# Two groups of leftover products in one PE block: eight PSUM banks in layer 1 of a CIN kernel

## The chip, the cores and the metric

The kernel runs on one core of one Trainium2 chip. The metric is the device time of one execution in microseconds. The kernel before took 2045.8 us (median of four runs, 2045.0 to 2046.51). All times below are microseconds unless another unit stands beside them. Engines are named as the profile names them: PE is the matrix engine, PEld its weight loads, DVE the vector engine (VectorE), ACT the scalar engine (ScalarE), POOL is GpSimd, SP is the queue that issues most loads.

## The reference

Two layers of a compressed interaction network over 4096 rows of 32 fields with 16 elements each. Each layer forms all products of two sets of fields, element by element, multiplies them by a weight matrix, adds a bias, and normalises each output channel over rows and elements. Half of the first layer's channels feed the second layer; everything else is summed over the elements.

```python
def _cin_layer(out, x, W, b, gamma, beta):
    r, _, e = x.shape
    h = jnp.einsum('rne,rfe->rnfe', out, x).reshape(r, -1, e)
    h = jnp.einsum('rce,oc->roe', h, W) + b[None, :, None]
    return _batchnorm(h, gamma, beta)      # mean and variance over rows and elements
h1 = _cin_layer(x, x, W1, b1, g1, beta1)   # W1: 128 x (32*32)
out, direct1 = (h1[:, :64], h1[:, 64:])
direct2 = _cin_layer(out, x, W2, b2, g2, beta2)   # W2: 128 x (64*32)
return jnp.concatenate([direct1, direct2], axis=1).sum(axis=-1)
```

Everything is in 32-bit floats.

## The kernel before, in words

The 65,536 sites (row and element) are cut into 128 tiles of 512. Layer 1 runs over the tiles, the last four (`ENDING`) in a part of their own; layer 2 runs over 64 chunks of two tiles, each in four stages.

**Layer 1, one tile.** A product x_i * x_j occurs twice, so only half of the products is formed, with the two weights added beforehand. 512 of them make the main part: two loads `a` and `b` on SP (512 KB each, four buffers each), one DVE multiplication into `z` (128 x 2048, L387, four buffers), four PE matmuls of 128 rows (L428). 16 products per tile are left over. The leftovers of eight tiles (`GROUP`) share one load `r` (L279) and one DVE product `zr` (L373), one buffer each; 16 rows of `zr` belong to each tile. Two tiles share a strip of 32 rows, and weights with 16 rows of zeros (`w1_sb[rows, 4]` or `[rows, 5]`) pick the one that is meant. `add_leftovers` (L376 to L382) issues four matmuls of 32 rows, one for each of four tiles, each into another bank.

**Order on PE.** At every fourth tile t four banks are taken from the pool `psum` (six banks); the block of leftovers begins the sums of tiles t to t+3, and the four main matmuls of each tile end them. Only the first two tiles (`FIRST`) begin with their main part and end with the leftovers.

**Eviction.** `finish(t)` (L342 to L361) is called one tile later: ACT evicts a bank three times (L352, L355, L358: all channels to `e`, the kept half to `h`, the direct half to `ed`), DVE takes statistics of `e` (L115, two `e` buffers), after each second tile also a sum of `ed` (L364), and ACT's queue stores `h` to HBM. Two more banks (the pool `factors`) are free in layer 1.

**Work for later.** A table (`EARLY`, L205 to L214) puts at fixed tiles the loads, negations and sums that prepare layer 2: two loads `xs` (L190) in every 24 tiles, layer 2's first operands from tile 75 on. The layer 2 weights come at tile 6 and are combined at tile 20.

**Order of the instructions.** A scheduler sets the order of each engine, by the order of the program and its own estimate of times; each engine then runs its own in that order, and waits on semaphores for the others. `tc.issue_after` binds an instruction behind another. SP issues DMAs in order as well, and a DMA waits for its buffer and for the one issued eight DMAs before.

**The beginning.** Tile 0 is loaded in four quarters. ACT's queue loads the weights `w1` and their mirror `w1m`, 384 KB each; POOL adds them in four steps (L312), the first main weights first. Tiles 0 and 1 are multiplied in four chunks each (L396).

**The boundary.** The last four tiles take their kept half first (L461), whose statistics give the scale and shift (`keep`) of layer 2's input. The direct half follows on PE while these are worked out, and the leftovers of the last four tiles use the last `zr`.

**Layer 2.** In a stage DVE multiplies twice (L667), adds one `t2` half (L662); POOL makes the other `t2` half (L703) and two differences `t14` (L714); PE makes 32 matmuls (L698). `combine` is a generator that evicts a chunk's sums in steps; `next(steps)` puts one step into the order of ACT and DVE.

Of the kernel before, what the change touches and what calls it, by code (L numbers as in the profile page):

```python
# [38 lines left out]
FP = mybir.dt.float32  # L42
# [4 lines left out]
P = 128  # L47
# [20 lines left out]


@with_exitstack  # L70
def tile_cin(ctx: ExitStack, tc: tile.TileContext, xa, xb, xr, w1, w1m, w2, bn, out):
    nc = tc.nc

    const = ctx.enter_context(tc.tile_pool(name="const", bufs=1))
# [188 lines left out]
    with ExitStack() as one:  # L263
# [11 lines left out]
        def load_rem(g):  # L275

            r = rpool.tile([P, 2 * T], FP, tag="r", name="r")
            with tc.issue_after(loads[-1].ins) if loads else nullcontext():
                nc.sync.dma_start(r, bass.AP(xr.tensor, xr.offset + g * P * 2 * T, [[2 * T, P], [1, 2 * T]]))  # L279
            return r  # L280

        def load_main(t):
            a = lpool.tile([P, 2 * T], FP, tag="a", name="a")
            b = lpool.tile([P, 2 * T], FP, tag="b", name="b")

            def load(to, part, n):
                at = part * T
                if to is a:
                    at += xa.offset + t * FIELDS * 2 * T
                    source = bass.AP(xa.tensor, at, [[2 * T, FIELDS], [0, 4], [1, n * T]])  # L290
                else:
                    at += xb.offset + (t * WRAP + 2) * T
                    source = bass.AP(xb.tensor, at, [[T, FIELDS], [4 * T, 4], [1, n * T]])
                return nc.sync.dma_start(to[:, part * T : (part + n) * T], source)

            if t == 0:

                parts = ((a, 0, 1), (b, 0, 1), (b, 1, 1), (a, 1, 1))
            else:
                parts = ((a, 0, 2), (b, 0, 2))  # L300
            for part in parts:
                last = load(*part)
            loads.append(last)
# [12 lines left out]
        neg_sb = const.tile([P, 2, 2, KEEP], FP, tag="neg", name="neg_sb")  # L316
# [46 lines left out]
        def sum_direct(c):  # L363
# [4 lines left out]
                ALU.add,  # L368
            )

        def leftovers(r):
            zr = rpool.tile([P, T], FP, tag="zr", name="zr")
            nc.vector.tensor_tensor(zr, r[:, :T], r[:, T:], ALU.mult)  # L373
            return zr

        def add_leftovers(t, zr, begun=0):  # L376

            for k in range(4):
                rows = slice(32 * k, 32 * (k + 1))
                nc.tensor.matmul(  # L380
                    pss[t + k], w1_sb[rows, 4 + t % GROUP // 4, :], zr[rows, :], start=k >= begun, stop=k < begun
                )  # L382

        def multiply_main(z, a, b, k):

# [11 lines left out]

        ending = NT - ENDING
        main = [load_main(t) for t in range(FIRST)]
        r = load_rem(0)  # L400
        for t in range(NT - ENDING):
            s = t % GROUP
            if s == 4 and t + 4 < NT:
                r = load_rem(t // GROUP + 1)
            if FIRST <= t + 1 < NT:
                main.append(load_main(t + 1))
            if s == 0 and t > 0:
                zr = leftovers(r)
            z = zpool.tile([P, 2, 2, T], FP, tag="z", name="z")
            if t < FIRST:  # L410
                for k in range(2):
                    for j in range(2):
                        product = multiply_chunk(z, *main[0], k, j)
            else:

                for k in (slice(0, 1), slice(1, 2)) if t == FIRST else (slice(0, 2),):
                    product = multiply_main(z, *main[0], k)
            main.pop(0)
            if t == FIRST - 1:
                with tc.issue_after(product.ins):  # L420
                    zr = leftovers(r)
            if s % 4 == 0:
                for k in range(4):
                    pss[t + k] = psum.tile([P, T], FP, tag="ps", name="ps")
            if s % 4 == 0 and t > 0:
                add_leftovers(t, zr)
            for m in range(4):
                nc.tensor.matmul(  # L428
                    pss[t],
                    w1_sb[:, m, :],  # L430
                    z[:, m // 2, m % 2, :],
                    start=t < FIRST and m == 0,
                    stop=t >= FIRST and m == 3,
                )
            if t == FIRST - 1:
                add_leftovers(0, zr, FIRST)
# [23 lines left out]
        def matmul(ps, w, z, start, stop):  # L460
            queue("pe", lambda: nc.tensor.matmul(ps, w, z, start=start, stop=stop))  # L461
# [13 lines left out]
        def add_leftovers_halves(banks, zr, direct, begun):  # L475

            for k in range(ENDING):
                rows = slice(32 * k, 32 * (k + 1))
                to = banks[k][half_of[(k + direct) % 2]]
                matmul(to, w1_sb[rows, 5, half_of[direct]], zr[rows, :], k not in begun, k in begun)  # L480
# [219 lines left out]
    def sum_first(z):  # L700

        t2 = tpool.tile([P, 2, T], FP, tag="t2", name="t2")
        queue("pool", lambda: nc.gpsimd.tensor_tensor(t2[:, 0], z[:, 1, 0], z[:, 0, 0], ALU.add))  # L703
        return t2

    def sum_rest(z, b11, t2, by_q, by_k):
# [149 lines left out]
    for c in range(NC):  # L856
# [3 lines left out]
        for k, i in enumerate(STAGES):  # L860
# [148 lines left out]
```

## Time and profile before

| what | value |
|---|---|
| median of four runs | 2045.8 (2045.0 to 2046.51) |
| the profiled execution | 2045.3, span 2043.6, mean granted PE clock 0.998 |
| PE, DVE, POOL, ACT busy | 2027.4, 1958.7, 1486.9, 1185.4 |
| layer 1 up to the last four tiles | from 0 to 474.3 |
| the last four tiles | 474.3 to 490.7 |
| layer 2 on PE | 490.7 to 2025.9 |

The page's first part gives busy time and share of each engine. PE is busy 99% of the span, and the chain that ended last is PE's by 98%, so the time is the sum of PE's work and what little PE waits. A line of the timeline reads: start, duration, engine, line of the kernel, operation, output <- inputs, shapes, count, and in brackets how long the engine stood idle before and what released it. A line of the chain reads: start, duration, engine, output, line, count. A line of the windows gives for each engine the busy time and the number of instructions, then the granted clock, the mean busy share of the 16 DMA engines (a little over 1 when they are full) and GB/s.

### The profile page before, as it was taken

How to read it: one execution, taken by the hardware profiler on the slowest of the kernel's cores; microseconds unless marked ns; L12 is line 12 of the kernel's file. 1: busy time of each engine (PE TensorE's matmuls, PEld its weight loads, DVE VectorE, ACT ScalarE, POOL GpSimd, SP SyncE). 2: the span in 40 equal slices, each digit the busy share in tenths (PEclk: the TensorE clock that was granted, in tenths of full speed). 3: DMA queues.
4: the chain of work that ended last, by engine and by line, in shares of the span. 5: the costliest groups of instructions: out<-in, count | busy, mean ns of one | idle time of the engine just before them, and what ended most of it. 6: DMA issues, size and time to landing. Idle time of an engine off the chain costs nothing.

```text
span 2043.6 us, 24467 instructions
## 1 busy us (share of the span) xinstructions
PE 2027.4 (99%) x8500; PEld 888.8 (43%) x8500; DVE 1958.7 (96%) x1521; ACT 1185.4 (58%) x1914; POOL 1486.9 (73%) x525
## 2 busy tenths in 40 slices
PE   9999999999999999999999999999999999999997
PEld 3444444443344444444444444444444444444443
DVE  8998987998999999999999999999999999999997
ACT  4555554554566666655666656556656565566564
POOL 0000000002999999999999999999999999999996
PEclk9999999999999999999999999999999999999999
DMA  9999999996777777777776777777777677777761
GB/s 391 376 354 365 343 362 339 380 386 190 174 179 174 178 175 180 189 174 183 179 177 166 174 174 176 177 181 178 176 166 174 174 172 182 181 176 176 168 162 42
DMA packets 112380, 440.70 MB, mean 216 GB/s; under 512 B 13056, under 2 KB 13056, under 8 KB 103808
## 3 DMA queue, kind: packets, MB, share of 16 engines
q1 hardware_dynamic: 105840, 418.43, 73.9%
q10 hardware_dynamic: 6416, 20.72, 2.6%
q8 instruction: 66, 1.08, 0.2%
q14 instruction: 58, 0.48, 0.1%
HBM read 417.07 MB, written 22.02 MB: 215 GB/s over the span
## 4 chain that ended last, share of the span: by engine, by line
PE 98%; DVE 1%; issue 0%; POOL 0%; DMA 0%; ACT 0%; DVEq 0%; ACTq 0%; POOLq 0%
PE x L698 74%; PE ps L428 21%; PE ps L380 2%; PE ps L461 1%; DMA w1m_sb<-in_w1m 0%; POOL t L714 0%; DVE zz L667 0%; DVE d L934 0%; ACT u L659 0%; DVE both L662 0%; POOL t L703 0%; ACT both L659 0%; DVE d L833 0%; DVE t L662 0%; POOL w_sb L312 0%
## 5 line engine op out<-in xcount | busy, mean ns | idle before, releaser
L714 POOL TENSOR_TENSOR t<-zz,t 128x2048 f32<-128x2048 f32 (+1 forms) x260 | 1164.0, 4478 | 20.8 <-DVE t L662 1.0
L698 PE MATMUL x<-t,s_sb 128*64 128x512 f32 x2040 | 958.3, 592 | 0.4 <-POOL t L714 0.4
L698 PE MATMUL x<-zz,s_sb 128*64 128x512 f32 x2048 | 935.0, 592 | 0.0
L698 PE MATMUL x<-zz,w_sb 128*64 128x512 f32 x2056 | 760.5, 592 | 0.0
L703 POOL TENSOR_TENSOR t<-zz 128x512 f32<-128x512 f32 x255 | 326.3, 1280 | 516.1 <-DVE zz L667 515.8
L667 DVE TENSOR_TENSOR zz<-f,bx 128x2048 f32<-128x2048 f32 x255 | 582.4, 2284 | 19.7 <-ACT f L659 19.7
L659 ACT ACTIVATE f<-a,keep 128x512 f32<-128x512 f32 x512 | 398.4, 778 | 342.8 <-DVE zz L667 293.1
L667 DVE TENSOR_TENSOR zz<-f,b 128x2048 f32<-128x2048 f32 x255 | 582.5, 2284 | 0.1
L698 PEld LDWEIGHTS x<-t,s_sb 128*64 128x64 f32 x2040 | 279.2, 137 | 485.0 <-issue 456.8
L698 PE MATMUL x<-t,w_sb 128*64 128x512 f32 x1020 | 479.3, 592 | 0.0
L428 PE MATMUL ps<-z,w_sb 128*128 128x512 f32 x992 | 434.7, 596 | 1.7 <-POOL w_sb L312 1.5
L698 PEld LDWEIGHTS x<-zz,s_sb 128*64 128x64 f32 x2048 | 279.5, 137 | 245.9 <-issue 239.3
L387 DVE TENSOR_TENSOR z<-a,b 128x2048 f32<-128x2048 f32 (+1 forms) x127 | 288.0, 2269 | 43.2 <-DMA b<-in_xb 21.3
L428 PEld LDWEIGHTS ps<-z,w_sb 128*128 128x128 f32 x992 | 185.7, 190 | 249.2 <-issue 228.1
L698 PEld LDWEIGHTS x<-zz,w_sb 128*64 128x64 f32 x2056 | 239.4, 137 | 120.8 <-issue 118.9
L659 ACT ACTIVATE b<-zz 128x512 f32<-128x512 f32 x255 | 152.4, 598 | 187.2 <-DVE zz L667 187.2
L352 ACT ACTIVATE e<-ps,bn_sb 128x512 f32<-128x512 f32 x124 | 85.2, 687 | 215.7 <-PE ps L428 162.0
L662 DVE TENSOR_TENSOR t<-zz,b 128x512 f32<-128x512 f32 x255 | 173.4, 680 | 0.4
L698 PEld LDWEIGHTS x<-t,w_sb 128*64 128x64 f32 x1020 | 139.6, 137 | 0.0
L596 ACT ACTIVATE unread<-e,center 128x512 bf16<-128x512 f32 x122 | 86.2, 707 | 0.0
L358 ACT ACTIVATE ed<-ps,bn_sb 64x512 f32<-64x512 f32 x124 | 84.7, 683 | 2.4
L115 DVE BATCH_NORM_STATS2 stats<-e 128x6 f32<-128x512 f32 x124 | 84.9, 686 | 0.0
(103 smaller groups left out, 867.1 us busy)
## 6 DMA issues: line engine op xcount, KB each, us to landing
a<-h SPq DMA_DIRECT2D x256, 512.0 KB, 4.6
b<-in_xb SPq DMA_DIRECT2D x64, 1024.0 KB, 9.4
a<-in_xa SPq DMA_DIRECT2D x127, 512.0 KB, 7.0
b<-in_xb SPq DMA_DIRECT2D x127, 512.0 KB, 8.1
bx<-in_xb SPq DMA_DIRECT2D x64, 512.0 KB, 9.3
bx<-x SPq DMA_DIRECT2D x64, 512.0 KB, 10.9
h<-kept ACTq DMA_DIRECT2D x64, 256.0 KB, 5.7
r<-in_xr SPq DMA_DIRECT2D x16, 512.0 KB, 8.7
```

The source lines that it names most:

```text
L115: nc.vector.bn_stats(self.stats[:, self.at, :], h)
L352: nc.scalar.activation(e, ps, AF.Identity, bias=b1)
L358: done = nc.scalar.activation(ed[to, :], ps[KEEP:, :], AF.Identity, bias=b1[KEEP:])
L387: return nc.vector.tensor_tensor(z[:, k], a.rearrange("p (a t) -> p a t", a=2)[:, k].unsqueeze(2).to_broadcast([P, n, 2, T]), b.rearrange( ...
L428: nc.tensor.matmul(pss[t], w1_sb[:, m, :], z[:, m // 2, m % 2, :], start=t < FIRST and m == 0, stop=t >= FIRST and m == 3,)
L596: return nc.scalar.activation(unread, e[:, s], AF.Square, bias=center[:, s], accum_out=squares[:, s, c : c + 1])
L659: return queue("act", lambda: nc.scalar.activation(to, source, AF.Identity, **scale_bias))
L662: return dve(lambda: nc.vector.tensor_tensor(to, x, y, ALU.add))
L667: dve(lambda: nc.vector.tensor_tensor(z, a, b.rearrange("p (k q) t -> p k q t", k=2), ALU.mult))
L698: queue("pe", lambda: nc.tensor.matmul(self.of[x], w, b, start=start, stop=stop))
L703: queue("pool", lambda: nc.gpsimd.tensor_tensor(t2[:, 0], z[:, 1, 0], z[:, 0, 0], ALU.add))
L714: queue("pool", lambda: nc.gpsimd.tensor_tensor(t14[:, k, q], z[:, 2 + k.start : 2 + k.stop, q], twice[:, k, q], ALU.subtract))
```

## The change

**Leftovers of eight tiles in one block.** At tiles 8, 16, ..., 120 (and no longer at 4, 12, ...) `add_leftovers` is called twice: it ends the sums of tiles t-4 to t-1 and begins those of t to t+3. Tiles 8g+4 to 8g+7 therefore begin with their main matmuls and are complete only when the double block of the next group has run. Both fours use one `zr`; the host arranges `xr` anew, so that a group holds tiles 8g-4 to 8g+3, in 17 groups and not 16. Tiles 6 and 7 of each eight take their banks from `factors`, so layer 1 uses all eight banks.

**Later eviction.** `finish` is called four tiles after a tile and not one; near the end twice in one tile, so that it catches up.

**The end of layer 1.** The last four tiles need a load `r` (at tile 121) and a `zr` of their own.

**The beginning.** Tile 0 comes in two loads as every other tile. ACT's queue loads the main weights and their mirror in one DMA (512 KB), SP the leftovers' weights (256 KB) behind tile 1's loads. DVE adds the main weights in one instruction, POOL the leftovers' weights.

**Layer 2.** For the stage (0, 1) DVE and not POOL makes the first half of `t2`. In chunks 0 to 4 one `next(steps)` of the first stage moves from behind the next stage's first factor to ahead of it.

```diff
@@ load_main
-            if t == 0:
-                parts = ((a, 0, 1), (b, 0, 1), (b, 1, 1), (a, 1, 1))
-            else:
-                parts = ((a, 0, 2), (b, 0, 2))
...
+            nc.sync.dma_start(
+                a, bass.AP(xa.tensor, xa.offset + t * FIELDS * 2 * T, [[2 * T, FIELDS], [0, 4], [1, 2 * T]])
+            )
+            at_b = bass.AP(xb.tensor, xb.offset + (t * WRAP + 2) * T, [[T, FIELDS], [4 * T, 4], [1, 2 * T]])
+            loads.append(nc.sync.dma_start(b, at_b))
@@ weights
-        w1m_sb = zpool.tile([P, 6, P], FP, tag="z", name="w1m_sb")
-        nc.scalar.dma_start(w1_sb, w1)
-        nc.scalar.dma_start(w1m_sb, w1m)
-        for k in (slice(0, 1), slice(1, 2), slice(2, 4), slice(4, 6)):
-            nc.gpsimd.tensor_tensor(w1_sb[:, k], w1_sb[:, k], w1m_sb[:, k], ALU.add)
+        w1_both = zpool.tile([P, 2, 4, P], FP, tag="z", name="w1_both")
+        nc.scalar.dma_start(w1_both, w1)
         bn_sb = load_bn()
+        left_both = zpool.tile([P, 2, 2, P], FP, tag="z", name="left_both")
+        nc.vector.tensor_tensor(w1_sb[:, :4], w1_both[:, 0], w1_both[:, 1], ALU.add)
@@ leftovers and banks
+        def multiply_leftovers(zr, r):
+            return nc.vector.tensor_tensor(zr, r[:, :T], r[:, T:], ALU.mult)
+        def bank(t):
+            pool, tag = (psum, "ps") if t % GROUP < 6 else (factors, "f")
+            return pool.tile([P, T], FP, tag=tag, name="ps")
+        def ends_with_leftovers(t):
+            return t % GROUP >= 4 or t < FIRST
-        def add_leftovers(t, zr, begun=0):
+        def add_leftovers(t, zr):
             for k in range(4):
                 rows = slice(32 * k, 32 * (k + 1))
-                nc.tensor.matmul(
-                    pss[t + k], w1_sb[rows, 4 + t % GROUP // 4, :], zr[rows, :], start=k >= begun, stop=k < begun
-                )
+                last = ends_with_leftovers(t + k)
+                w = w1_sb[rows, 4 + (t + 4) % GROUP // 4, :]
+                nc.tensor.matmul(pss[t + k], w, zr[rows, :], start=not last, stop=last)
@@ the loop over tiles
         main = [load_main(t) for t in range(FIRST)]
+        nc.sync.dma_start(left_both, w1_left)
+        nc.gpsimd.tensor_tensor(w1_sb[:, 4:], left_both[:, 0], left_both[:, 1], ALU.add)
         r = load_rem(0)
...
-                    pss[t + k] = psum.tile([P, T], FP, tag="ps", name="ps")
-            if s % 4 == 0 and t > 0:
+                    pss[t + k] = bank(t + k)
+            if s == 0 and t > 0:
+                add_leftovers(t - 4, zr)
                 add_leftovers(t, zr)
...
-            if t > 0 and t < ending - 1:
-                evicted = finish(t - 1)
+            if t >= ending - 2:
+                evicted = finish(t - 2)
+            elif t >= ending - 4:
+                for done in range(2 * t - ending, 2 * t - ending + 2):
+                    evicted = finish(done)
+            elif t >= 4:
+                evicted = finish(t - 4)
+            if t == ending - 3:
+                r = load_rem(NT // GROUP)
...
-            if t == 0:
+            if t < 4:
                 continue
@@ the last four tiles
+            if k == 0:
+                zr = rpool.tile([P, T], FP, tag="zr", name="zr")
+                queue("dve", lambda: multiply_leftovers(zr, r))
@@ layer 2
-                t2 = sum_first(z)
+                t2 = sum_first(z, (c, k) == (0, 1))
...
+            if k == 0 and c < 5:
+                next(steps, None)
...
-            next(steps, None)
+            if k > 0 or c >= 5:
+                next(steps, None)
@@ the host
-    xr = np.stack([xt[:, :16], xt[:, 16:]], axis=2).reshape(NT // GROUP, GROUP // 4, 4, 16, 2, T)
+    xr = np.stack([xt[:, :16], xt[:, 16:]], axis=2)
+    xr = np.concatenate([xr[:4], xr, xr[-4:]]).reshape(NT // GROUP + 1, GROUP // 4, 4, 16, 2, T)
```

More of the change, by code (lines that the diff above doesn't have):

```diff
@@ L70, in tile_cin @@
 @with_exitstack
-def tile_cin(ctx: ExitStack, tc: tile.TileContext, xa, xb, xr, w1, w1m, w2, bn, out):
+def tile_cin(ctx: ExitStack, tc: tile.TileContext, xa, xb, xr, w1, w1_left, w2, bn, out):
     nc = tc.nc
@@ L284, in load_main @@
             b = lpool.tile([P, 2 * T], FP, tag="b", name="b")
[L286 to L290, printed above, removed]
-                else:
-                    at += xb.offset + (t * WRAP + 2) * T
-                    source = bass.AP(xb.tensor, at, [[T, FIELDS], [4 * T, 4], [1, n * T]])
-                return nc.sync.dma_start(to[:, part * T : (part + n) * T], source)
-            if t == 0:
-                parts = ((a, 0, 1), (b, 0, 1), (b, 1, 1), (a, 1, 1))
-            else:
-                parts = ((a, 0, 2), (b, 0, 2))
-            for part in parts:
-                last = load(*part)
-            loads.append(last)
+            nc.sync.dma_start(
[3 more added lines that the diff above has]
+            loads.append(nc.sync.dma_start(b, at_b))
             return a, b
         w1_sb = wpool.tile([P, 6, P], FP, tag="w1", name="w1_sb")
-        w1m_sb = zpool.tile([P, 6, P], FP, tag="z", name="w1m_sb")
-        nc.scalar.dma_start(w1_sb, w1)
-        nc.scalar.dma_start(w1m_sb, w1m)
-        for k in (slice(0, 1), slice(1, 2), slice(2, 4), slice(4, 6)):
-            nc.gpsimd.tensor_tensor(w1_sb[:, k], w1_sb[:, k], w1m_sb[:, k], ALU.add)
+        w1_both = zpool.tile([P, 2, 4, P], FP, tag="z", name="w1_both")
+        nc.scalar.dma_start(w1_both, w1)
         bn_sb = load_bn()
+        left_both = zpool.tile([P, 2, 2, P], FP, tag="z", name="left_both")
+        nc.vector.tensor_tensor(w1_sb[:, :4], w1_both[:, 0], w1_both[:, 1], ALU.add)
         w2_sb = const.tile([P, 16, P], FP, tag="w2", name="w2_sb")
@@ L369, in sum_direct @@
             )
+        def multiply_leftovers(zr, r):
+            return nc.vector.tensor_tensor(zr, r[:, :T], r[:, T:], ALU.mult)
         def leftovers(r):
             zr = rpool.tile([P, T], FP, tag="zr", name="zr")
[L373 removed]
+            multiply_leftovers(zr, r)
             return zr
[L376 removed]
+        def bank(t):
[4 more added lines that the diff above has]
+        def add_leftovers(t, zr):
             for k in range(4):
                 rows = slice(32 * k, 32 * (k + 1))
[L380 to L382 removed]
+                last = ends_with_leftovers(t + k)
+                w = w1_sb[rows, 4 + (t + 4) % GROUP // 4, :]
+                nc.tensor.matmul(pss[t + k], w, zr[rows, :], start=not last, stop=last)
         def multiply_main(z, a, b, k):
@@ L431, in tile_cin @@
                     z[:, m // 2, m % 2, :],
-                    start=t < FIRST and m == 0,
-                    stop=t >= FIRST and m == 3,
+                    start=ends_with_leftovers(t) and m == 0,
+                    stop=not ends_with_leftovers(t) and m == 3,
                 )
             if t == FIRST - 1:
-                add_leftovers(0, zr, FIRST)
-            if t > 0 and t < ending - 1:
-                evicted = finish(t - 1)
+                add_leftovers(0, zr)
+            if t >= ending - 2:
[7 more added lines that the diff above has]
+                r = load_rem(NT // GROUP)
             if t == 20:
@@ L479, in add_leftovers_halves @@
                 to = banks[k][half_of[(k + direct) % 2]]
-                matmul(to, w1_sb[rows, 5, half_of[direct]], zr[rows, :], k not in begun, k in begun)
+                matmul(to, w1_sb[rows, 4, half_of[direct]], zr[rows, :], k not in begun, k in begun)
         zs = []
@@ L698, in matmul, with sum_first @@
             queue("pe", lambda: nc.tensor.matmul(self.of[x], w, b, start=start, stop=stop))
-    def sum_first(z):
+    def sum_first(z, at_once):
         t2 = tpool.tile([P, 2, T], FP, tag="t2", name="t2")
-        queue("pool", lambda: nc.gpsimd.tensor_tensor(t2[:, 0], z[:, 1, 0], z[:, 0, 0], ALU.add))
+        if at_once:
+            add(t2[:, 0], z[:, 1, 0], z[:, 0, 0])
+        else:
+            queue("pool", lambda: nc.gpsimd.tensor_tensor(t2[:, 0], z[:, 1, 0], z[:, 0, 0], ALU.add))
         return t2
@@ L967 @@
     xb = xt[:, np.arange(WRAP) % FIELDS]
-    xr = np.stack([xt[:, :16], xt[:, 16:]], axis=2).reshape(NT // GROUP, GROUP // 4, 4, 16, 2, T)
-    xr = xr.transpose(0, 2, 1, 3, 4, 5).reshape(NT // GROUP, P, 2, T)
+    xr = np.stack([xt[:, :16], xt[:, 16:]], axis=2)
+    xr = np.concatenate([xr[:4], xr, xr[-4:]]).reshape(NT // GROUP + 1, GROUP // 4, 4, 16, 2, T)
+    xr = xr.transpose(0, 2, 1, 3, 4, 5).reshape(NT // GROUP + 1, P, 2, T)
     w1nf = w1.reshape(P, FIELDS, FIELDS)
@@ L987 @@
             w1m[32 * q + 16 * u + lo, 4 + u] = w1nf[:, lo + 16, lo].T
+    w1_both = np.stack([w1t, w1m], axis=1)
     w2t = np.ascontiguousarray(w2.reshape(P, 4, 16, 8, 4).transpose(2, 3, 1, 4, 0)).reshape(P, 16, P)
@@ L994 @@
     arrays, args = {}, []
-    for name, a in (("xa", xa), ("xb", xb), ("xr", xr), ("w1", w1t), ("w1m", w1m), ("w2", w2t), ("bn", bn)):
+    for name, a in (("xa", xa), ("xb", xb), ("xr", xr), ("w1", w1_both[:, :, :4]), ("left", w1_both[:, :, 4:]), ("w2", w2t), ("bn", bn)):
         a = np.ascontiguousarray(a)
```

## The prediction

> **What bounds the kernel now.** I read the page's first two parts (who is busy, and when), the chain as pieces in order of time, single instructions in the timeline, and last DMA by stretch and by load.
>
> ```profile
> span 2043.6 us, 24467 instructions
> PE 2027.4 (99%) x8500; PEld 888.8 (43%) x8500; DVE 1958.7 (96%) x1521; ACT 1185.4 (58%) x1914; POOL 1486.9 (73%) x525
> 324.34 1.07 PE ps L380 x8
> 325.41 13.93 PE ps L428 x32
> 339.35 1.07 PE ps L380 x8
> 340.42 13.93 PE ps L428 x32
> ```
>
> PE never rests. In layer 1 the chain is PE alone with a period of 15.00 us (339.35 - 324.34): one block of leftovers (L380), then four tiles (L428).
>
> ```profile
> 40.85 0.19 PEld L428 LDWEIGHTS ps<-z,w_sb 128*128 128x128 f32 x1 [0.24 <-issue]
> ...
> 44.28 0.19 PEld L428 LDWEIGHTS ps<-z,w_sb 128*128 128x128 f32 x1 [0.24 <-issue]
> 84.25 1.14 PE L380 MATMUL ps<-zr,w_sb 32*128 32x512 f32 x8
> 85.32 1.56 PE L428 MATMUL ps<-z,w_sb 128*128 128x512 f32 x3
> ```
>
> Each fp32 matmul appears as two passes. Between 40.85 and 44.28 lie eight passes, 0.429 each, so a tile is 8 x 0.429 = 3.43. The four row groups of a block run together and cost two passes: 34 x 0.429 = 14.59 of the 15.00. The other 0.41 is paid per block for going from 128 rows to 32 and back.
>
> ```profile
> 330.97 2.29 DVE L387 TENSOR_TENSOR z<-a,b 128x2048 f32<-128x2048 f32 x1 [2.40 <-DMA b<-in_xb]
> 335.90 2.29 DVE L387 TENSOR_TENSOR z<-a,b 128x2048 f32<-128x2048 f32 x1 [2.04 <-DMA b<-in_xb]
> 341.99 2.29 DVE L387 TENSOR_TENSOR z<-a,b 128x2048 f32<-128x2048 f32 x1 [2.60 <-DMA b<-in_xb]
> 344.80 2.28 DVE L387 TENSOR_TENSOR z<-a,b 128x2048 f32<-128x2048 f32 x1
> 349.32 2.29 DVE L387 TENSOR_TENSOR z<-a,b 128x2048 f32<-128x2048 f32 x1 [1.06 <-DMA b<-in_xb]
> 355.93 2.29 DVE L387 TENSOR_TENSOR z<-a,b 128x2048 f32<-128x2048 f32 x1 [3.71 <-DMA b<-in_xb]
> 355.35 4.99 PE L428 MATMUL ps<-z,w_sb 128*128 128x512 f32 x11
> 324.00:354.00 30.00, 30.00 (x81) 12.62 (x80) 20.11 (x17) 13.56 (x21) 0.00 (x0) 1.00 1.03 323
> r<-in_xr SPq DMA_DIRECT2D x1, 512.0 KB, 11.1
> ```
>
> These are the products of tiles 88 to 93. PE takes tile 92 at 355.35, so tile 93 at 355.35 + 3.43 + 0.1 = 358.88, and its product is ready at 358.22: 0.66 to spare. In quiet stretches it is some 9, the four z buffers (z of tile 48 ends at 181.36, PE takes that tile at 190.33). The cover is eaten by loads: in 324 to 354 VectorE is busy only 20.11 of 30 while DMA is full (1.03) at 323 GB/s; the fullest stretch reaches 421. The last line is the load of r for tiles 96 to 103, issued at 341.53, landed at 352.6.
>
> **The change, part by part.** The profiled execution took 2045.3 (span 2043.6 and 1.7 around it), 0.5 under the median of 2045.8; the sum is made against it.
>
> *Blocks of eight.* 31 blocks become 1 + 15. The passes stay, 15 x 0.41 = 6.2 go. Between the fours of a double block the next weights go into the same row groups. From below, that hides as the second pass of a four does today: 84.25 to 85.32 holds both passes with one exposed load; cost 0. From above it is a full switch, 0.41 each, and the gain is nil. I take 0, as the row is the same form on the same row groups. [...]
>
> *Late eviction.* Tiles 8g+4..8g+7 end only in the double block at the start T of tile 8g+8. In the changed program VectorE's order there is: z(8g+11), four statistics with two direct sums and the next zr among them, and only then z(8g+12). Rows: z 2.2 from start to the next instruction's, each small one 0.6, ScalarE 1.98 per tile (0.69 + 0.67 + 0.69, pipelined). The fourth tile's statistics cannot start before T + 1.0 + 3 x 1.98 + 0.7 = T + 7.6; its direct sum ends at T + 9.9, z(8g+12) at T + 12.2. PE wants it at T + 2.14 + 4 x 3.43 = T + 15.86 (2.14 is four passes and 0.41). So with prompt loads nothing is lost, but the cover at this tile is 3.7 and not 9. Banks are no limit: those of 8g+8..8g+11 were evicted in the previous group, over ten us earlier.
>
> *The dip at tile 88.* Fusing ten pairs, the block of tile 84 that now comes later (1.29) and the beginning (0.4) put T at 339.27 - 4.1 - 1.29 - 0.4 = 333.5. Do loads come earlier too? The load of tile 88 waits for z84's buffers; z84 ends at T(80) + 12.2, with T(80) = 309.3 - 3.7 - 1.29 - 0.4 = 303.9: 316.1, against 316.6 now. So no. With today's landings z90 ends at 344.3 where PE wants it at 333.5 + 2.14 + 6.86 = 342.5: stall 1.8. z91 ends at 347.1; three statistics and a sum take it to 349.5; zr waits for r until 352.6; with zr, a statistic, a sum and z92 it is 356.7. PE, at tile 90 from 344.3, wants tile 92 at 351.2: stall 5.5. Together 7.3. If all loads came 5.8 earlier it would be 1.4 (r at 346.8, z92 at 350.8 against 349.4). I take 7.3, because of z84. The same sum at tiles 76 and 84 ends 0.3 to 0.6 before PE's need (r issued at 274.4 and 304.7 lands 11.4 and 10.4 later), and at tile 13, where VectorE is still catching up and has one more zr and sum to do, about even: 0 to 4 for the three, I take 1.
>
> *Beginning.* ScalarE's queue loads 512 KB of weights instead of 768, SP brings 256 KB of leftover weights after tile 1, tile 0 comes whole, and VectorE adds the main weights (0.69). POOL's four adds, which spread tile 0 over 8.48 to 12.58 (4.10 for 3.43), go; its one add left, under 1.3, lies beside tile 1. So r and tile 2's loads stand behind 256 KB on SP that ScalarE's queue carried before: the same bytes ahead of them. The first chunk now needs 1.5 MB landed, as much as today lands by 8.34: PE starts between 8.1 and 9.1, tile 1 0.9 sooner to 0.1 later. I take -0.4.
>
> *End of layer 1.* One more r (512 KB on SP, before tile 123's loads, landed well before T) and one zr (0.6). The same order of VectorE gives z127 at T + 20.9, PE wants it at T + 15.87 + 1.05 + 3.5 = T + 20.5: +0.4, between 0 and 2. The statistics behind it keep their distance to the last tile, so the keep chain moves with PE.
>
> *Layer 2.* VectorE takes t2's first half once (0.6) from POOL (1.28); POOL's chain starts at most 0.7 sooner and PE's pause of 0.59 at 526.35 shrinks; the moved step puts three evictions into 1.6 us of ScalarE's idle time in five rounds. Between -0.6 and +0.3; I take -0.2. Everything else there is covered by PE's 1,535 us of gapless matmuls.
>
> Sum: -6.2 - 0.4 + 7.3 + 1.0 + 0.4 - 0.2 = +1.9: 2047.2 beside the profiled run, 2047.7 beside the median.
>
> **Rivals.**
> *The cover holds (faster).* The dip of 324 to 354 follows loads of other shapes and may be shallower under another rhythm. For it: most stretches show 5 to 9 us of cover. Against: the r load and z84. The dip at its lower bound and no other stall: -6.2 - 0.4 + 1.4 + 0.4 - 0.2 = -5.0, or -6.4 with no dip: 2039.4 to 2040.8.
> *The load queue starves (slower).* Loads of tile n wait for z(n-4), and in every group no z ends between T + 2.3 and T + 12.2. Four loads of 1.05 MB wait at most: at 420 GB/s they are done by about T + 7.5, then DMA stands for some 4.7. A group moves 8 x 1.05 + 0.5 + 4 x 0.26 = 10 MB, in 29.6 - 4.7 = 24.9 us 400 GB/s, just under 420; a group with 1 to 2 MB more (xs, layer 2's first operands) needs 440 to 480 and falls 1.2 to 3.6 behind. There are about six: +4 to +12 on top, 2051 to 2059, 2054 in the middle. It decides once stalls pass 10.5. For it: seven of the fourteen 30 us windows from 54 to 474 show a DMA share of 1.02 or more. Against: full share at 390 is not full speed.
> *The seam costs a full switch (the change does not do what it says).* +6.2: 2054. Against: the block's rows.
>
> **How the numbers follow.** Give-back 0.45 (own range 2043.5 to 2050.5), starving 0.31, cover holds 0.18, seam 0.06. About 0.2%, 4.1 us, is what a measurement tells from no change: 2041.7 to 2049.9. Faster is the covering case and a rim: 0.19. Same is the give-back less its rims: 0.43. Slower is starving, seam and the upper rim: 0.38. Leaving out half of the covering case (below 2040) and the top third of the slow ones (above 2055) is about 0.2: 2040 to 2055.
>
> **What would show it.** Right: double blocks of about 1.9 from first start to the next tile and a group period of 29.6; VectorE's z of tile 92 standing behind zr and that behind r; PE idle some 5 us once near 350, and little elsewhere. Wrong: double blocks of 2.3; PE idle in most groups with DMA idle shortly before (starving); no PE gap over 1 us after 20 (cover).

## The result, and the profile after

The changed kernel took 2047.38 (median of 36 executions, 2044.01 to 2057.52), the kernel before beside it 2046.28 (56 executions, 2044.93 to 2047.04). The ratio is 1.0011, with a 95% interval of 1.0006 to 1.0016: 0.1% slower, inside the 0.2% that were called no change. What changed most is the spread: 2.1 before, 13.5 after. The profiled execution took 2044.02, among the fastest, 3.4 under the median, so one profile is not enough to read this kernel; the experiments below add eleven. (One execution of one experiment, named `both`, took 4394, its matmuls of layer 2 at 1146 ns in the mean where the changed kernel has 592; it was the profiled one, so that run has times and no profile to read, and its ratio leaves it out.)

The page of the changed kernel, span and engines:

```profile
span 2042.3 us, 24485 instructions
PE 2025.0 (99%) x8500; PEld 890.6 (44%) x8500; DVE 1960.2 (96%) x1524; ACT 1185.8 (58%) x1914; POOL 1488.7 (73%) x521
```

The chain in order of time, around the place of the old blocks (start, duration, output, line, count):

```profile
334.32 1.93 PE ps L378 x16
336.25 27.66 PE ps L428 x64
363.91 1.93 PE ps L378 x16
365.84 27.66 PE ps L428 x64
```

The double block takes 1.93 from its first start to the next tile, where the single one took 1.07. The difference, 0.86, is two passes of 0.429 and nothing else: the seam between the fours is free. The period of a group is 363.91 - 334.32 = 29.59, against 2 x 15.00. The window of the predicted dip has PE without a pause and VectorE busy 24.71, not 20.11, of 30:

```profile
324.00:354.00 30.00, 30.00 (x83) 12.96 (x82) 24.71 (x22) 14.53 (x24) 0.00 (x0) 1.00 1.03 387
```

VectorE's timeline around z of tile 92 (the last line) in this execution:

```profile
338.64 2.29 DVE L383 TENSOR_TENSOR z<-a,b 128x2048 f32<-128x2048 f32 x1 [0.17 <-DMA b<-in_xb]
340.85 1.28 DVE L116 BATCH_NORM_STATS2 stats<-e 128x6 f32<-128x512 f32 x2
342.05 0.67 DVE L350 TENSOR_REDUCE d<-ed 128x32 f32<-128x512 f32 x1
342.63 0.68 DVE L116 BATCH_NORM_STATS2 stats<-e 128x6 f32<-128x512 f32 x1
345.62 0.69 DVE L358 TENSOR_TENSOR zr<-r 128x512 f32<-128x512 f32 x1 [2.31 <-DMA r<-in_xr]
346.23 0.69 DVE L116 BATCH_NORM_STATS2 stats<-e 128x6 f32<-128x512 f32 x1
346.84 0.67 DVE L350 TENSOR_REDUCE d<-ed 128x32 f32<-128x512 f32 x1
347.42 2.28 DVE L383 TENSOR_TENSOR z<-a,b 128x2048 f32<-128x2048 f32 x1
```

The order is the predicted one: z91, two statistics and a sum, a statistic, 2.31 of idle time for `r`, `zr`, a statistic, a sum, and only then z92. It ends at 349.71; PE takes tile 92 at 350.02, 0.31 later. So in this execution the dip costs nothing, by 0.31.

In layer 2 VectorE waits where it never waited before (timeline, then the sum over 495 to 610: time in total, times, longest):

```profile
510.33 2.29 DVE L678 TENSOR_TENSOR zz<-f,b 128x2048 f32<-128x2048 f32 x1 [0.48 <-ACT f L670]
...
536.80 2.29 DVE L678 TENSOR_TENSOR zz<-f,b 128x2048 f32<-128x2048 f32 x1 [0.87 <-ACT f L670]
```

```profile
DVE zz L678 <- ACT f L670: 3.2, 4, 0.9
```

ScalarE's timeline ahead of the first of these waits shows who is late:

```profile
507.59 0.59 ACT L670 ACTIVATE both<-x 64x512 f32<-64x512 f32 x1
508.20 0.68 ACT L670 ACTIVATE both<-x,b_swapped 64x512 f32<-64x512 f32 x1
508.89 0.59 ACT L670 ACTIVATE e<-x 64x512 f32<-64x512 f32 x1
509.51 0.78 ACT L670 ACTIVATE f<-a,keep 128x512 f32<-128x512 f32 x1
```

Three evictions of the combining step (`both` twice, `e`) stand ahead of the factor `f` that VectorE needs. In the kernel before, the factor came first (ScalarE's timeline there):

```profile
513.52 0.78 ACT L659 ACTIVATE f<-a,keep 128x512 f32<-128x512 f32 x1 [1.60 <-DVE zz L667]
514.33 0.59 ACT L659 ACTIVATE both<-x 64x512 f32<-64x512 f32 x1
```

Where the time went is seen best in the starts of the same matmul in two profiles. PE's lead over the kernel before (negative is earlier):

| place | before | after | lead |
|---|---|---|---|
| tile 2 | 17.18 | 16.33 | -0.85 |
| tile 120 | 460.36 | 454.55 | -5.81 |
| layer 2, first matmul | 490.67 | 485.82 | -4.85 |
| layer 2, 176 matmuls on | 529.13 | 523.93 | -5.20 |
| layer 2, 368 on | 570.34 | 567.89 | -2.45 |
| layer 2, last | 2030.48 | 2029.43 | -1.06 |

Up to tile 120 layer 1 gave nearly what fusing the blocks was to give, the last four tiles took 0.95 of it, and layer 2 took 3.8 in all: it won 0.35 up to 524 and lost 4.15 between 524 and 600.

### The profile page after: what moved, and what is told of

Its sections match the earlier page's. It is cut to its first block, busy times and chain, and to the rows that moved or that the text cites. A ratio compares the mean times of both kernels' runs of the same rounds, so it can differ in the third digit from the quotient of the medians.

```text
span 2042.3 us, 24485 instructions
## 1 busy us (share of the span) xinstructions
PE 2025.0 (99%) x8500; PEld 890.6 (44%) x8500; DVE 1960.2 (96%) x1524; ACT 1185.8 (58%) x1914; POOL 1488.7 (73%) x521
## 4 chain that ended last, share of the span: by engine, by line
PE 95%; DVE 3%; issue 1%; ACT 0%; POOL 0%; DMA 0%; DVEq 0%; SPq 0%; ACTq 0%; POOLq 0%
PE x L709 73%; PE ps L428 20%; PE ps L378 1%; DVE zz L678 1%; PE ps L469 1%; DVE z L383 1%; DMA b<-in_xb 0%; POOL t L728 0%; DVE d L847 0%; DVE t L673 0%; DVE stats L116 0%; DVE both L673 0%; DVE d L350 0%; ACT e L670 0%; ACT f L670 0%
```

## The experiments

Two theories were put to the test: that the moved step of layer 2 costs 3.8 by itself ("step"), and that the spread is the lost cover of z of tile 8g+12 in layer 1 ("cover", with `r` in front of it), each with rivals. Medians are of 11 executions, of 5 for the two last kernels. The experiments were run in three groups (the first four, the next four, the last four), and the kernel before, run beside each group, had 2046.34, 2045.88 and 2046.31. Ratios are to the kernel before of the same group.

**The moved step put back.** In the changed kernel:

```diff
-            if k == 0 and c < 5:
-                next(steps, None)
...
-            if k > 0 or c >= 5:
-                next(steps, None)
+            next(steps, None)
```

> The changed kernel with the moved step of layer 2 put back behind the next factor, nothing else. Theory 'step': in rounds 1 to 4 three evictions now stand on ScalarE ahead of the factor, VectorE, which is full there, waits 0.48, 0.87, 0.93 and 0.93 for it, and PE loses 3.8 of its lead of 4.85 between 538 and 600. Then the lead of about 5 stays to the end: 3 to 4 less than the changed kernel, a median of 2043.5 to 2044.5, and the fastest executions near 2040.5. Rival 'backlog': VectorE is full from 520 to 620 in both kernels, so its work sets the pace as soon as PE is ahead; then PE waits somewhere else in the same stretch and the gain is 0 to 1. The spread between executions comes from layer 1 and stays at some 10 under both.

Measured: 2047.49 (2042.3 to 2049.69), ratio 1.0002 (0.9993 to 1.0011). The fastest came down by only 1.7 and the median not at all; the time does not show the gain. The profile does: VectorE waits for ScalarE nowhere between 495 and 610, and PE's lead goes from -0.54 at layer 2's first matmul to -0.15 at its last, a loss of 0.39 where the changed kernel lost 3.79. The lead was small because this execution met the dip. VectorE's timeline, and PE's at tile 92:

```profile
341.68 2.29 DVE L383 TENSOR_TENSOR z<-a,b 128x2048 f32<-128x2048 f32 x1 [0.16 <-DMA b<-in_xb]
343.89 1.28 DVE L116 BATCH_NORM_STATS2 stats<-e 128x6 f32<-128x512 f32 x2
...
345.67 0.68 DVE L116 BATCH_NORM_STATS2 stats<-e 128x6 f32<-128x512 f32 x1
350.03 0.69 DVE L358 TENSOR_TENSOR zr<-r 128x512 f32<-128x512 f32 x1 [3.67 <-DMA r<-in_xr]
...
351.83 2.28 DVE L383 TENSOR_TENSOR z<-a,b 128x2048 f32<-128x2048 f32 x1
```

```profile
354.25 4.10 PE L428 MATMUL ps<-z,w_sb 128*128 128x512 f32 x9 [3.73 <-DVE z L383]
```

`r` lands at 349.94, VectorE has waited 3.67 for it, z92 ends at 354.11 and PE has been idle 3.73. Whether a lead of 5 is kept too was left to the later runs. Why the median of this run did not fall at all is not shown; that its executions met more half clocks in layer 1 is a guess, from 5 of 11 with a mean clock of 0.996, against 7 of 36 of the changed kernel.

**The moved step alone,** the same lines the other way round in the kernel before.

> The kernel before with the moved step of layer 2 alone. Theory 'step': VectorE loses the same 3.2 of its time and PE has no lead to pay with, so 3 to 4 slower: 2049.3 to 2050.3. Rival 'backlog' (the loss is only a lead that cannot be kept): within 0.5 of the kernel before, 2046.3.

Measured: 2049.78 (2048.72 to 2051.8), ratio 1.0019 (1.0010 to 1.0028), 3.4 by the medians. PE stands at 0.01 at layer 2's first matmul and 3.81 behind at its last. VectorE's waits between 495 and 610 (the line numbers are those of the kernel before):

```profile
DVE zz L667 <- ACT f L659: 3.6, 4, 0.9
```

"Step" holds, "backlog" falls: there was no lead to lose, and 3.8 went all the same.

**The leftovers' product behind z of tile 8g+15.** In the changed kernel:

```diff
             if s == 0 and t > 0:
-                zr = leftovers(r)
+                with tc.issue_after(product.ins):
+                    zr = leftovers(r)
```

> The changed kernel with the product of the leftovers queued on VectorE behind z of tile 8g+15 instead of ahead of z of tile 8g+12: the wait for r is taken from in front of z, the four statistics and two sums stay there. Theory 'r': it is r's landing that eats the 3.1 of cover in some executions; the spread falls from 13 to about 3 and the median by 2 to 3, to 2044.5 to 2045.5. Rival 'loads': the ordinary loads come too late in some executions, whatever stands behind r; the median falls by at most 0.6 (the shorter queue) and the spread stays over 8.

Measured: 2045.8 (2044.51 to 2056.41), ratio 1.0005 (0.9995 to 1.0015); nine of eleven between 2044.5 and 2048, seven under 2045.9. The profile has no gap of PE in layer 1 after the beginning; at tile 92, z is ready 0.78 ahead. `r` landed at 349.78 in it, as late as in the run with the step put back (349.94), where PE lost 3.73: with z ahead of the leftovers' product the late `r` cost nothing. The median is 1.6 below the changed kernel's and 0.3 above the range that "r" gave; the spread, 11.9 with one outlier, is what "loads" gave. The profiled execution, at 2047.01, shows something else, at the very start. PE's timeline, then the windows (PE, PEld, VectorE, ScalarE, POOL, granted clock, DMA share, GB/s):

```profile
1.55 4.29 PE L240 MATMUL begun<-ones 128*128 128x512 f32 x6 [1.55 <-DVE ones L237]
8.86 2.08 PE L429 MATMUL ps<-z,w_sb 128*128 128x512 f32 x2 [3.02 <-DVE z L392]
```

```profile
4.50:7.91 3.41, 1.34 (x3) 0.27 (x2) 0.69 (x1) 0.90 (x5) 0.00 (x0) 1.00 1.02 409
7.92:14.74 6.82, 5.88 (x7) 2.52 (x8) 6.12 (x9) 0.10 (x1) 1.25 (x1) 0.50 1.03 418
```

PE was idle for 3.02 between the matmuls on ones and tile 0, and the clock was half from 7.92 to 14.74. Tile 2 starts at 19.90 and not at 16.33; 0.66 of that is the later first tile, some 2.9 the clock.

**The statistics two tiles later as well.**

```diff
-            stats1.add(e)
...
-            if half == 1:
-                sum_direct(c)
+            late.append(lambda: (stats1.add(e), sum_direct(c) if half == 1 else None))
@@ finish, first lines
+            if len(late) == 2:
+                with tc.issue_after(product.ins):
+                    late.pop(0)()
```

> As the run before, and each tile's statistics and sum are queued two tiles later, behind z of the tile in hand, so that z of tile 8g+12 ends some 3 earlier against PE's need. Theory 'cover': what is left of the spread goes, because z leads PE by 6 to 9 everywhere, and z buffers and so loads come free earlier: a spread of 2 to 3, median 2044, fastest 2043, with the 4 of layer 2 still lost. Under 'loads' the median is 2045 to 2047 with a spread over 8, as in the changed kernel.

Measured: 2045.19 (2043.3 to 2048.18), ratio 0.9995 (0.9986 to 1.0004); the spread is 4.9, more than the 2 to 3 expected and less than the 13.5 of the changed kernel. The median is 1.2 above what "cover" gave and within the 2045 to 2047 of "loads", so the times alone do not decide. In the profile z of tile 76 is now ready 7.75 ahead, where the changed kernel had 3.13, and z of tile 92 3.09 ahead, where it had 0.31; but z of tile 93 only 0.51, so the cover is not 6 to 9 everywhere. PE has no gap in layer 1 up to tile 123. A new one of about 1 appears in the last four tiles, and layer 2 loses its 3.80.

**A longer prelude** (four matmuls on ones, not three).

```diff
-BEGIN = 3
+BEGIN = 4
```

> The changed kernel with four instead of three matmuls on ones ahead of the first tile, nothing else. One profile (of the run zr_late) shows the clock at 0.50 from 8 to 14.9 after PE had been idle for 3.0 between those matmuls and the first tile; the others, idle for 1.35 to 1.56, keep 1.00. Theory 'clock': part of the spread is this half clock at the start, in the executions whose mean clock is 0.997 or less (17 of 36 of the changed kernel): with the longer prelude PE is idle for under 1.5, nearly all executions have 0.998, those of 0.996 and less are gone, and the median falls by 1 to 2, to 2045.5 to 2046.5. Rival 'stalls': the low mean clocks follow the stalls of layer 1 at tile 92, not the start; the shares of the clocks and the median stay as they were, within 0.5 of 2047.4.

Measured: 2048.07 (2044.35 to 2051.38), ratio 1.0011 (1.0003 to 1.0020). The median did not fall, so "clock" at the start is not what sets it. Executions with a mean clock under 0.998 were 2 of 11, where the changed kernel had 17 of 36; but the kernel before, which has no stall in its profile, had 17 of 33 beside it, so that share does not count the changed kernel's half clocks. The profile (2047.8 of span) has PE at tile 0 at full clock, and PE is idle in layer 1 for 0.97 near 321 and for 2.20 near 352. Windows, columns as above:

```profile
350.29:353.70 3.41, 1.33 (x4) 0.26 (x2) 3.41 (x4) 3.35 (x6) 0.00 (x0) 1.00 1.03 420
353.70:357.11 3.41, 3.29 (x4) 1.51 (x5) 3.41 (x4) 2.32 (x4) 0.00 (x0) 0.50 1.03 417
```

With the second gap the clock is halved for four passes, from 353.7 to 357.1, which costs about 1.6 more (the six passes from 353.82 on take 4.44; at full clock, in the changed kernel run again below, six take 2.81). So a half clock can come from a stall too, as "stalls" has it; that the longer prelude keeps one away at the start is not shown.

**The new beginning alone,** in the kernel before.

```diff
-        nc.scalar.dma_start(w1_sb, w1)
-        nc.scalar.dma_start(w1m_sb, w1m)
-        for k in (slice(0, 1), slice(1, 2), slice(2, 4), slice(4, 6)):
-            nc.gpsimd.tensor_tensor(w1_sb[:, k], w1_sb[:, k], w1m_sb[:, k], ALU.add)
+        nc.scalar.dma_start(w1_both, w1)
...
+        nc.vector.tensor_tensor(w1_sb[:, :4], w1_both[:, 0], w1_both[:, 1], ALU.add)
...
+        nc.sync.dma_start(left_both, w1_left)
+        nc.gpsimd.tensor_tensor(w1_sb[:, 4:], left_both[:, 0], left_both[:, 1], ALU.add)
```

> The kernel before with the new beginning alone (weights in one load of 512 KB, leftover weights on SP behind the first two tiles, VectorE adding the main weights, tile 0 whole). My sum had -0.4 for it, between -0.9 and +0.1: 2045.4 to 2046.4. Profiles of the changed kernel put tile 2 at 16.33 instead of 17.18: -0.85, 2045.4. Rival 'clock': without POOL's adds in the way the first tile waits for its loads alone, and where they are late PE is idle longer and the clock halves for 6 us, which costs up to 3: a median of 2046.5 to 2048 with more executions at a clock of 0.996.

Measured: 2044.73 (2044.53 to 2046.89), 1.15 under the median beside it and 0.7 below the range that was expected; the ratio, 0.9998 (0.9989 to 1.0007), can't tell it from nothing. The median overstates it: the fastest executions differ by 0.3, and 8 of 11 executions, against 16 of 33 of the kernel before, had the higher mean clock of 0.998 and with it the lower times. The profile has PE 0.71 ahead at layer 2's first matmul and at its last, 0.46 of it from an earlier first tile. The sign is that of the sum, the size lies between 0.3 and 0.7; no execution shows the loss that "clock" warned of.

**Both repairs** (the step put back, and the cover).

> Both repairs on the changed kernel: the moved step of layer 2 put back, and the leftovers' product and late statistics queued behind z. Theory 'step': layer 2 keeps the whole lead of about 5, since before_step lost 3.8 without any lead: 3.8 less than the kernel with the cover alone, fastest executions 2039.5 to 2040, median 2041 to 2041.5. Rival 'backlog': VectorE, full from 520 to 620, cannot hold a lead of 5 whatever the order; some 2 of it are lost there again, fastest 2041.5 to 2042, median 2043.

Measured: 2041.28 with the one named above counted, 2041.16 without it (2039.91 to 2043.97), ratio 0.9979 (0.9970 to 0.9988): 4.0 less than with the cover alone, which lost 3.80 in layer 2. With it goes the same kernel with four matmuls on ones:

> Both repairs and the longer prelude. 'Step', 'cover' and 'clock' together: a median of 2040 to 2041 and a spread under 3, faster than both kernels. If 'clock' falls it is as the run with both repairs.

Measured: 2040.53 (2039.83 to 2046.37), ratio 0.9976 (0.9967 to 0.9985), ten of eleven within 1.7. Its profile holds a lead of 4.94 at layer 2's first matmul and 4.55 at its last. "Backlog" is gone for good: a lead of 5 is kept. What the longer prelude adds, 0.6 between the medians of two kernels with such spreads, is not settled.

**The changed kernel again.**

> The changed kernel once more, as the baseline of this call and for one more profile of layer 1. Expected as before: a median of 2046 to 2049.5 and a spread of 6 or more. If its profile is of an execution over 2046, PE is idle at tile 84 or 92, VectorE waits for r there just before, and the clock is halved for some 3.4 after one of these gaps (theory 'r behind the early loads'). Rival 'start': the lost time lies before 20.

Measured: 2048.65 (2046.06 to 2053.53), ratio 1.0014 (1.0005 to 1.0023). Its profile is of an execution of 2046.0 of span, VectorE's timeline first, then PE's at tiles 84 and 92:

```profile
317.30 0.69 DVE L358 TENSOR_TENSOR zr<-r 128x512 f32<-128x512 f32 x1 [3.94 <-DMA r<-in_xr]
...
349.40 0.69 DVE L358 TENSOR_TENSOR zr<-r 128x512 f32<-128x512 f32 x1 [2.85 <-DMA r<-in_xr]
```

```profile
322.45 2.81 PE L428 MATMUL ps<-z,w_sb 128*128 128x512 f32 x6 [2.09 <-DVE z L383]
```

```profile
353.62 2.81 PE L428 MATMUL ps<-z,w_sb 128*128 128x512 f32 x6 [1.34 <-DVE z L383]
```

VectorE waits 3.94 and 2.85 for `r`, and PE 2.09 and 1.34 for the z behind it. The start is not to blame (tile 0 at 7.96). No half clock followed these two gaps (the granted clock is 1.00 from 320 to 352, and six passes take 2.81 after either), so that part of the expectation failed.

**Layer 2's early loads four tiles later,** away from the loads of `r`.

```diff
-EARLY += [(75, lambda: early.append(load_b(0))), (83, lambda: early.append(load_bx(0)))]
-EARLY += [(91 + 8 * k, lambda i=i: ...) for k, i in enumerate(STAGES)]
+EARLY += [(79, lambda: early.append(load_b(0))), (87, lambda: early.append(load_bx(0)))]
+EARLY += [(95 + 8 * k, lambda i=i: ...) for k, i in enumerate(STAGES)]
```

> The changed kernel with the loads of layer 2's first operands four tiles later (tile numbers 75, 83, 91, 99, 107, 115 become 79, 87, 95, 103, 111, 119): they no longer stand right ahead of the loads of r (tiles 76, 84, 92, ...) on SP's queue, nothing else moves. Theory 'r behind the early loads': r lands 1.2 earlier at tile 92 (512 KB at 420 GB/s) and 2.4 at tile 84, so the gap at 84 goes and that at 92 falls from 4 to under 3; the median falls by 1 to 3 against the changed kernel in this call and comes near that of the run with the leftovers' product moved (2045.8). Rival 'bytes': what counts is how much is loaded in layer 1, not what stands ahead of r; then the median is within 0.5 of the changed kernel's, or the gaps move to other tiles.

Measured: 2049.57 (2047.88 to 2053.96), ratio 1.0019 (1.0011 to 1.0028), 0.9 above the changed kernel beside it. `r` for tile 84's place lands at 312.54 and not at 317.21, and the gap there is gone, as expected; but the changed kernel's first profile, with `r` at 313.01, had none there either. At tile 92 (VectorE, then PE):

```profile
337.05 2.29 DVE L383 TENSOR_TENSOR z<-a,b 128x2048 f32<-128x2048 f32 x1 [4.72 <-DMA b<-in_xb]
341.36 2.29 DVE L383 TENSOR_TENSOR z<-a,b 128x2048 f32<-128x2048 f32 x1 [2.01 <-DMA b<-in_xb]
...
348.86 0.69 DVE L358 TENSOR_TENSOR zr<-r 128x512 f32<-128x512 f32 x1 [0.37 <-DMA r<-in_xr]
...
351.38 2.28 DVE L383 TENSOR_TENSOR z<-a,b 128x2048 f32<-128x2048 f32 x1
```

```profile
353.80 6.66 PE L428 MATMUL ps<-z,w_sb 128*128 128x512 f32 x11 [2.97 <-DVE z L383]
```

`r` is hardly waited for now (0.37). The products of tiles 89 and 90 wait for their own loads, 4.72 and 2.01: two loads `bx` now stand among those of `xs`, at tiles 86 and 88, and the late work is pushed on to z92 all the same. The theory that the place ahead of `r` sets the time fell here: the median did not come down. That "bytes" is right instead is argued and not shown: its median was off as well (0.9, not 0.5), and no run loads less into that stretch.

**The end of layer 1.** In the kernel with both repairs and the longer prelude PE waits, near the end, for ScalarE's evictions of the kept half, and these stand behind one that waited for a statistic (PE's, then ScalarE's timeline):

```profile
476.53 4.36 PE L478 MATMUL ps<-z,w_sb 128*64 128x512 f32 x16 [0.87 <-ACT kept L523]
```

```profile
471.83 0.69 ACT L346 ACTIVATE e<-ps,bn_sb 128x512 f32<-128x512 f32 x1 [7.11 <-DVE stats L116]
```

```diff
@@ after the loop over the tiles of layer 1
+        late.pop(0)()
```

> Both repairs and the longer prelude, and at the end of layer 1 the statistics of tile 120 go out ahead of the last three z instead of behind them. In the run without this, ScalarE's evictions of tiles 122 and 123 wait 7.1 for that (to 471.83), the next evictions come late, and PE loses 0.87 and a slipped pair at 475.7. If that is the cause the gap of 1.46 there goes: 0.9 to 1.0 less, a median of 2039.5 and fastest 2038.9. If z of tile 127 then ends too late instead, the gap stays, some 2.5 earlier, and the median is 2040.5 as before.

Measured: 2038.91 (2038.66 to 2039.57), ratio 0.9963 (0.9951 to 0.9976), a spread of 0.9; the gap is gone, and the lead at layer 2's first matmul is 6.80, at its last 6.41. Of the 1.86 won, 0.58 is an earlier first tile in that execution (7.88, not 8.46), so the edit is worth about 1.3.

```profile
span 2036.9 us, 24481 instructions
PE 2021.8 (99%) x8502; PEld 891.0 (44%) x8502; DVE 1959.5 (96%) x1524; ACT 1185.5 (58%) x1914; POOL 1482.6 (73%) x521
```

**`t2` back on POOL,** in that kernel (`sum_first(z, False)`).

> As the run before, with the other edit of layer 2 undone: the first half of t2 of the second stage back on POOL. My sum had -0.2 for both edits of layer 2 together. By the profiles PE's lead grows by 0.35 to 0.6 at 527, where it waits for POOL's t in the kernel before: undoing it costs 0.3 to 0.6, a median of 2039.9 to 2040.1. If the edit is worth nothing, the two are within 0.1.

Measured: 2038.9 (2038.49 to 2044.43), ratio 0.9968 (0.9955 to 0.9980): no difference in the medians, though the profiles show one. With VectorE's `t2` half the lead is 6.80 at first, 6.52 after 160 matmuls, 7.10 after 176 and 6.41 by 600; without it, it stays at 6.21 from first to last. The edit wins 0.58 where PE waited for POOL, and loses 0.28 before it and 0.65 to 0.7 after it: 0.39 in all, so undoing it helps by the profiles and does not cost the 0.3 to 0.6 expected. In these two profiles an earlier first tile (7.88, not 8.48) hides that.

PE's lead over the kernel before at layer 2's first and last matmul, in all these profiles:

| kernel | moved step | first | last | lost in layer 2 |
|---|---|---|---|---|
| changed kernel | yes | -4.85 | -1.06 | 3.79 |
| changed kernel again | yes | -1.18 | 2.62 | 3.80 |
| step alone, in the kernel before | yes | 0.01 | 3.81 | 3.80 |
| product of leftovers later | yes | -1.88 | 1.92 | 3.80 |
| cover | yes | -5.14 | -1.34 | 3.80 |
| longer prelude | yes | 0.65 | 4.45 | 3.80 |
| early loads shifted | yes | 0.70 | 4.50 | 3.80 |
| step put back | no | -0.54 | -0.15 | 0.39 |
| both repairs, longer prelude | no | -4.94 | -4.55 | 0.39 |
| the same, end repaired | no | -6.80 | -6.41 | 0.39 |
| the same, `t2` on POOL | no | -6.21 | -6.21 | 0.00 |
| new beginning, in the kernel before | no | -0.71 | -0.71 | 0.00 |

## Why the prediction was right, and where it was not

The forecast was 2047.7, the time 2047.38, on the side of no change that it named the likeliest. That the two numbers agree is luck: in the profiled execution the dip cost 7.3 less than the sum has for it and layer 2 4.0 more, and the median lies 3.4 above that execution.

- **Blocks of eight, -6.2.** Right. From tile 2 to tile 120 the changed kernel is 4.96 faster, with 0.8 lost at tile 13 and 0.2 at tile 3 in it, and the seam costs nothing. The rival with a full switch at the seam is out: it wanted double blocks of 2.3, and 1.93 was measured.
- **Late eviction.** The mechanism was right in each step (order on VectorE, z behind `zr` behind `r`). Cover of z of tile 8g+12 was put at 3.7 with prompt loads; the profile has 3.13 at tiles 28, 52 and 76.
- **The dip at tile 88, +7.3.** Right in place, too large in size, and not one number but a distribution: 0 in the profiled execution, and at tile 92 1.34, 2.20, 2.97 and 3.73 in the four other profiles that have `zr` ahead of z92 (2.97 with the shifted loads), with about 1.6 more in the two where the clock was halved after it. `r` landed at 345.53 in the first, at 349.94 in the worst; I had 352.6 from the kernel before. The step that failed is the choice of the upper bound "because of z84", that loads would come no earlier: `r` came earlier by 3 to 7. The lower bound, with loads 5.8 earlier, was the better end for the profiled execution.
- **Tiles 13, 76 and 84, +1.** 0.8 at tile 13 in the changed kernel's profile; at tile 84 nothing there, and idle times of 2.09 and 0.97 in two others.
- **Beginning, -0.4.** Small as forecast: -0.85 at tile 2, -0.71 alone in the profiles, 0.3 between the fastest executions, inside its bounds of -0.9 to +0.1. The half clock after a late first tile was not in the sum at all.
- **End of layer 1, +0.4.** 0.95, inside 0 to 2. z of tile 127 ends at 473.84, PE wanted it at 472.98.
- **Layer 2, -0.2.** Wrong: +3.8. The step that failed is "the moved step puts three evictions into 1.6 us of ScalarE's idle time", with the rest put under "PE's 1,535 us of gapless matmuls". ScalarE's 1.6 before the factor was there, but the three evictions take 1.9 and stand ahead of a factor that VectorE takes at once, and VectorE has no idle time between 520 and 600 in the kernel before (busy 80.00 of 80). Each wait of 0.48 to 0.93 put VectorE back for good, and from 538 on PE with it. The `t2` half that VectorE took over lost 0.39 in the profiles without the moved step, where a gain had been expected.
- **Rivals.** "The load queue starves" in every group did not happen: in the profiles, PE's gaps of over 0.3 between tile 2 and the last four tiles stand at tiles 13, 84 and 92 only. "Cover holds" is what the profiled execution shows in layer 1; without the moved step it would have been at 2040.6 (2044.02 - 3.79 + 0.39, from the last table), in the range of that rival.

Left open: why one execution lands its loads 4 later than another at the same tile, what made the outliers of the kernels with z put first (2056.41, 2046.37, 2044.43), and how much of the spread is half clock. An estimate for the last: a half clock of 3.41 lowers the mean clock of some 2045 by 0.0008 and costs about 1.6, so the slowest execution, at 0.994 against 0.998, had some five of them, give or take one, about 8 of the 13.5.

## What to carry to other kernels

Cost a moved instruction on the engine that is full, not on the one that it runs on: idle time of ScalarE is no cover when the next instruction of a full VectorE waits behind it (here 3.2 of such waits, and PE 3.8 later). Where a gain is paid for with cover, read the price in the spread and look at several executions; here the price in layer 1 was bookkeeping (statistics, a product that is needed 18 us later) queued ahead of the next operand. With the operand first (2.2 less), the step of layer 2 put back (4.0 less), one more matmul on ones and the end of layer 1 repaired, the changed kernel's 2047.38 became 2038.91. A saving on PE is kept to the end only if the engine that feeds the following stage is not pushed back in the same edit: here 4.85 at the first matmul of layer 2 were 1.06 at its last.

## What the runs showed of the hardware

- The clock of PE was halved after idle times of 3.02 (the later product, at the start; half for 6.82), 2.20 (the longer prelude; half for 3.41) and 2.97 (the shifted loads; told from the eleven passes after it, 6.66, where the kernel before takes 4.88 from 454.47 on). It was not halved after 2.09 (the changed kernel again) and 3.73 (the step put back), the longest of all. The windows around that gap (PE's busy time is the first number behind the comma):

```profile
348.88:352.30 3.42, 1.64 (x4) 0.38 (x2) 2.27 (x4) 1.72 (x3) 0.00 (x0) 1.00 1.03 420
352.30:355.71 3.41, 1.46 (x4) 0.77 (x5) 3.41 (x3) 3.06 (x6) 0.00 (x0) 1.00 1.02 417
```

  PE is idle for 1.78 in the first of them and 1.95 in the second, and the granted clock is 1.00 in both. The windows further up that end where the clock was halved have 2.07 (the later product) and 2.08 (the longer prelude). So the length of a gap alone does not tell whether the clock falls; what does is not shown by five gaps. A half clock in layer 1 cost 1.6 to 1.8: six passes in 4.44 against 2.81, eleven in 6.66 against 4.88.
- A block of 32-row matmuls twice as long cost its passes and no more: 1.07 to 1.93, two passes of 0.429. What a group takes beside its passes was 0.41 with the single block (15.00 less 34 passes) and 0.42 with the double one (29.59 less 68).
